# A pre-norm transformer block in fp32 on one core: the last 96 hidden features on four column tiles, and one batch's rows transposed through DRAM

## The chip, the core and the metric

The kernel runs on one core of a Trainium2 chip. Time is device microseconds (us) of one execution. The kernel before was run three times: 890.35, 890.20 and 889.15 us, median 890.2 us. One further execution was taken with the profiler; it lasted 889.38 us, of which 887.7 us lie between the first and the last instruction (the span).

## The reference, cut to what matters

```python
B, T, D = 4, 512, 512          # resid; 32 query heads and 8 key heads of 16; FF = 1376
x = resid
h = layernorm(x)
q, k, v = h @ Wq, h @ Wk, h @ Wv            # rotary embedding on q and k
probs = softmax(causal(q @ k.T / 4))        # four query heads share a key head
x = x + (probs @ v) @ Wo
h = layernorm(x)
x = x + (silu(h @ W_gate.T) * (h @ W_up.T)) @ W_down.T
```

All of it is fp32. The feed-forward layer has F = 1376 = 10 x 128 + 96 hidden features, so the last block of features is 96 wide.

## The kernel before, in words

**Layout.** A projection needs the normalised rows with features on the partitions (`xnT`, 128 x 4 x 512, one for a batch of 512 rows). There are two ways to turn rows round. `transposed` (L255) lets PE transpose four 128x128 blocks into a bank of PSUM, which ACT or DVE copies out. `flipped` (L265) lets DVE transpose 32x32 blocks of a 128x512 tile (`xt`, L268), then sends the tile to a DRAM buffer with four DMAs (L272) and brings finished columns back with one DMA for each 128 rows (L274); the call for the last row tile issues two such reads. All these DMAs are issued by SP, in program order, and so are the loads of input rows (L338, four of 256 KB for a batch), the writes and reads of row maxima (L640, L649, L651), and the feed-forward weights (L161).

**Attention.** Work goes in 32 groups, eight a batch: four heads that share the 32-row strips of PE. A group is computed twice: "plain" scores (queries on partitions, L553), of which DVE takes the greatest of each row (L599), and, two groups later, "less" scores (keys on partitions, L566) from which the maximum has been subtracted, for ACT's exponential (L654), POOL's causal mask (L659) and PE's weighted averages (`av`, L681). `slot(b, steps)` (L799) runs the eight groups of batch b. In one turn for group g it does five visits: visits n = 0 to 3 of the loop (L827) and `last_visit` (L848). Each visit issues plain scores of group g+2 and less scores of group g on PE, then the reduction of the plain scores on DVE; the next visit's plain scores use the same PSUM banks. Maxima are turned by DVE (L639) and go through DRAM.

**What fills the gaps.** `slot` also gets a list of steps (`steps`): PE work of the neighbouring batches, each with a planned cost, which `gap(n)` hands out after each visit by shares of the total. Small DVE, ACT and POOL steps wait in a queue `aside`; `odd_steps` (L225) hands them out after each visit's reductions, as many as fit a planned budget. For layernorm of batches 2 and 3 these are, for each of four row tiles: measure m (L200 to L203), normalise n (a small DVE step, L210, then ACT, L211) and flip f, in the order m0 m1 n0 m2 f0 n1 m3 f1 n2 n3 f2 f3 (L324). A step `tail(i)` (L414, the lists `turned`) makes sure that flip i has been handed out, by handing out from `aside` until it has. `begin` (L406) of a batch issues that batch's four input loads and appends its twelve steps to `aside`.

**Which batch turns how.** Batches 1 and 3 are flipped through DRAM buffer `flip[1]`; batches 0 and 2 are transposed by PE (the flag `b % 2`). Batch 2's layernorm is queued in the opening, before slot 0; in slot 0 the list is: rest of batch 1's projections with the four transposes of batch 2 woven into their last eight steps (`turns`, L880), then `begin3`, batch 2's projections, the waits for batch 3's flips, and most of batch 3's projections. `xt` tiles and the feed-forward's `g` tiles share two buffers (tag "g").

**Feed-forward.** `hidden(b, n)` (L483) computes, for each block f of features, two halves: gate (a = 0) and up (a = 1). A half is four products (contraction over 4 x 128 features) of `m` output features by 512 rows. In the slots `narrow` is set, and `product_of` (L248) splits a product into column tiles of 32 output features; after slot 3 (batch 3's feed-forward) a product is one 128-column matmul. For f = 10 the block is 96 wide, so three column tiles of 512 columns are used. An fp32 matmul appears in the trace as two passes. Gating is a tanh on ACT (L503) and two DVE operations (L504, L506) into `home`; `down` (L512) multiplies by W_down, block f = 10 last. `hidden` of batches 0, 1 and 2 runs in slots 1, 2 and 3 as filler.

Of the kernel before, what the change touches and what calls it, by code (L numbers as in the profile page):

```python
# [14 lines left out]
AF = mybir.ActivationFunctionType  # L15
ALU = mybir.AluOpType
# [5 lines left out]
P = 128  # L22
# [52 lines left out]
def preln_block_kernel(  # L75
# [172 lines left out]
    def product_of(out, lhsT, rhs, start, stop):  # L248
        if not narrow[0]:
            nc.tensor.matmul(out, lhsT=lhsT, rhs=rhs, start=start, stop=stop)  # L250
            return
        for c in range(0, out.shape[0], 32):
            nc.tensor.matmul(out[c : c + 32], lhsT=lhsT[:, c : c + 32], rhs=rhs, start=start, stop=stop)  # L253
# [11 lines left out]
    def flipped(xn, i, n, dst, last=NT - 1):  # L265

        t = work.tile([P, D], F32, tag="g", name="xt", bufs=2)
        nc.vector.transpose(t, xn)  # L268
        turned = flip[n].rearrange("(c d) (i r s) -> i r d c s", d=32, r=4, s=32)
        for r in range(4):  # L270
            rows = t[32 * r : 32 * r + 32, :]
            nc.sync.dma_start(out=turned[i, r], in_=rows.rearrange("d (c s) -> d c s", s=32))  # L272
        for a in [i - 1, i] if i == last else [i - 1] if i > 0 else []:
            nc.sync.dma_start(out=dst[:, :, ts(a, P)], in_=flip[n].rearrange("(k p) t -> p k t", p=P)[:, :, ts(a, P)])  # L274

    def portions(products, finish, n=2):

        made = {}

        def part(a):  # L280
            if a == 0:
                made["ps"] = bank()
            for step in products[len(products) * a // n : len(products) * (a + 1) // n]:
                step(made["ps"])
            if a == n - 1:
                full.append(deque(finish(made["ps"])))
                if not thin[0]:
                    emptied(len(full))

        return [lambda a=a: part(a) for a in range(n)]  # L290
# [22 lines left out]
    def both_steps(measure, norm, flip, tiles=range(NT), norm_us=0.6, flip_us=0.75):  # L313

        for i in tiles:
            yield 1.05, lambda i=i: measure(i)
            for a in [i - 1, i] if i == NT - 1 else [i - 1] if i > 0 else []:
                yield norm_us, lambda a=a: norm(a)
                yield flip_us, lambda a=a: flip(a)

    def both_steps_apart(measure, norm, flip, flip_us):

        steps = {"m": (1.05, measure), "n": (0.2, norm), "f": (flip_us, flip)}
        for kind, i in ("m0", "m1", "n0", "m2", "f0", "n1", "m3", "f1", "n2", "n3", "f2", "f3"):  # L324
            cost, step = steps[kind]
            yield cost, lambda step=step, i=int(i): step(i)

    def projections(b, n, early=False, then=None):

        home, xa, found, xn, ready = homes[n], {}, {}, {}, []  # L330
        xnT = xnT_of[b]

        def load(i):
            if early:
                xa[i] = xr[b, i]
            else:
                xa[i] = work.tile([P, D], F32, tag="xa", name="xa", bufs=4)
                nc.sync.dma_start(out=xa[i], in_=x[b, ts(i, P), :])  # L338

        def measure(i):  # L340
            found[i] = statistics(xa[i])

        def norm(i):
            xn[i] = work.tile([P, D], F32, tag="xa", name="xa", bufs=4) if early else xa[i]
            normalised(xn[i], found[i], by_act=b > 1)

        def flip(i):
            if b > 1:
                release()
            if b % 2:  # L350
                flipped(xn[i], i, 1, xnT)
            ready.append(i)
            if i == NT - 1 and then:
                then()

        def keys():
            def finish(ps):
                kr = work.tile([P, T], F32, tag="rot", name="kr", bufs=4)

                def spread():  # L360
                    release()
                    ks = work.tile([P, T], F32, tag="rot", name="ks", bufs=4)
                    nc.vector.stream_shuffle(ks, kr, SWAP)
                    for t, hf, src in ((0, 0, kr), (1, 1, kr), (0, 1, ks), (1, 0, ks)):
                        put(
                            lambda t=t, hf=hf, src=src: nc.gpsimd.tensor_scalar(
                                home[:, 4 + 2 * t + hf, :], src, halves[hf], (one16, one0)[hf], ALU.mult, ALU.add
                            )
                        )

                last = spread if early else lambda: soon.append((1, (0.75, spread)))
                return [*rotated(ps, kr, nc.vector if early else nc.gpsimd), (0.0, last)]

            return projected(wk_sb, 0, xnT, finish)

        def vals():
            def product(ps, i, k):
                for c in (0, 64) if i == NT - 1 else ():
                    token = P * i + 64 - c
                    product_of(  # L380
                        ps[c : c + 64, ts(i, P)], xnT[:, k, token : token + 64], wv_sb[:, k, :], k == 0, k == NK - 1
                    )
                if i < NT - 1:
                    product_of(ps[:, ts(i, P)], xnT[:, k, ts(i, P)], wv_sb[:, k, :], k == 0, k == NK - 1)

            def finish(ps):
                def copy():
                    nc.scalar.copy(
                        values(n)[:, :, :, DH : 2 * DH].rearrange("p i g d -> p (i g) d"),
                        ps.rearrange("p (a d) -> p a d", d=DH),  # L390
                    )

                return [(0.0, copy)]

            steps = [lambda ps, i=i, k=k: product(ps, i, k) for i in range(NT) for k in range(NK)]
            return [(0.45, step) for step in portions(steps, finish, 8)]

        def queries(m):
            engine = nc.vector if early and m == 0 else nc.gpsimd
            return projected(wq_sb, m, xnT, lambda ps: rotated(ps, home[:, m, :], engine))  # L400

        def load_all():
            for i in range(NT):
                load(i)

        def begin():  # L406
            if not xa:
                load_all()
            if b > 1:
                aside.extend(both_steps_apart(measure, norm, flip, 0.75 if b % 2 else 0.0))  # L410
            else:
                aside.extend(both_steps(measure, norm, flip, flip_us=0.75 if b % 2 else 0.0))

        def tail(i):  # L414
            while i not in ready:
                do(aside)
            if b % 2 == 0:
                transposed(xn[i], i, xnT)

        turned = [(0.0 if b % 2 else 0.45, lambda i=i: tail(i)) for i in range(NT)]  # L420
        rest = [*keys(), *queries(0), *vals()]
        for m in range(1, 4):
            rest += queries(m)
        return (0.0, begin), turned, rest, load_all
# [58 lines left out]
    def hidden(b, n):  # L483

        gs = {}

        def half(f, a):
            c = b * NF + f
            m = min(P, FF - f * P)

            def product(ps, k):
                if a == 0 and k == 0:
                    load_f(c + 2)
                product_of(ps[:m, :], wgu[c][:, a, k, :m], xnTs[0][:, k, :], k == 0, k == NK - 1)

            def finish(ps):
                return [(0.69, lambda: gated(ps))]

            def gated(ps):
                if a == 0:  # L500
                    gs[f] = work.tile([P, T], F32, tag="g", name="g", bufs=2)

                    nc.scalar.activation(gs[f][:m, :], ps[:m, :], AF.Tanh, scale=0.5)  # L503
                    nc.vector.scalar_tensor_tensor(gs[f][:m, :], gs[f][:m, :], 1.0, ps[:m, :], ALU.add, ALU.mult)  # L504
                else:
                    nc.vector.tensor_tensor(homes[n][:m, f, :], ps[:m, :], gs[f][:m, :], ALU.mult)  # L506

            return [(1.72, step) for step in portions([lambda ps, k=k: product(ps, k) for k in range(NK)], finish)]

        return [step for f in range(NF) for a in range(2) for step in half(f, a)]  # L510

# [365 lines left out]
    def restored():  # L877
        nc.scalar.dma_start(out=homes[1], in_=spill)

    turns = [step for pair in zip(turned2, *[iter(rest1[-8:])] * 2) for step in pair]  # L880
    slot(0, [*rest1[16:-8], *turns, begin3, *rest2, *turned3, *rest3[:-24]])

    before, behind = attended(0, by_pe=(2, 3))
    tiles = list(down(0, 0))
# [62 lines left out]
```

## Time and profile before

| what | value |
|---|---|
| median of three runs | 890.2 us (889.15 to 890.35) |
| the profiled execution | 889.38 us, span 887.7 us |
| PE, DVE, POOL, ACT busy | 865.9, 469.6, 233.7, 204.5 us |
| granted TensorE clock | 1.000 by the profile |
| chain of work that ended last | PE 81%, DVE 12%, POOL 3%, issue 2%, DMA 1%, ACT 1% |
| transposes by DVE for DRAM (L268) | 22, 0.71 us each |
| transposes by PE (L258) | 40, of these 16 for batch 2, at 79.1, 85.5, 88.2 and 90.8 us |
| first statistics of batch 3 (L200) | 95.69 us, right behind the DVE work before it |

How to read it: a line of the timeline gives start, duration, engine, line, operation, out<-in, shape and count, and in brackets how long the engine was idle and what ended that. "128*32 128x512" is a matmul with 128 rows of contraction, 32 output features and 512 columns. PE's ends are modelled, so starts are safer than ends. An SP line (SPq) is the time that SP took to issue DMAs, not the transfer.

First reductions of the groups in slot 0 (L599, 128x512) start at 51.58, 69.40, 85.65, 100.75, 116.17, 131.48, 147.65 and 162.75 us; slot 1 begins at 178.92 us. Slots 1 to 3 last until about 730 us, then follows batch 3's feed-forward.

### The profile page before, as it was taken

Reading aid. Unit: us, or ns where it says so; the run is one execution under the profiler, and the core shown is the slowest. Engines: PE = TensorE matmul, PEld = TensorE weight load, DVE = VectorE, ACT = ScalarE, POOL = GpSimd, SP = SyncE. Lnnn points to the kernel's source line nnn. Section 1 sums busy time; section 2 is a strip of 40 time slices with the busy share of each in tenths; the row PEclk is TensorE's granted clock in tenths of the full one; section 3 lists DMA queues with packets and bytes.
Section 4 is the critical chain, followed back from the end, with each engine's and each line's share of the span. In section 5 each row is a group of like instructions: output and inputs, shape, how many; then the busy total and the mean of one; then the engine's idle time right before and its main releaser. Section 6 shows DMA issues by size and latency. Waiting matters only on the chain.

```text
span 887.7 us, 23915 instructions
## 1 busy us (share of the span) xinstructions
PE 865.9 (98%) x10142; PEld 352.0 (40%) x10142; DVE 469.6 (53%) x1481; ACT 204.5 (23%) x256; POOL 233.7 (26%) x358
## 2 busy tenths in 40 slices
PE   6989999999999999999999999999999999999998
PEld 5654444544333333333333333333333334444443
DVE  7886788777555554485555544575555214121110
ACT  1024433322323222222222222122222220000100
POOL 5564475653212211132221122222211211000000
PEclk9999999999999999999999999999999999999999
DMA  8500114005515110524221110142111203523000
GB/s 247 133 5 4 52 16 87 4 4 121 180 50 178 44 50 14 192 51 110 55 57 50 31 40 25 52 98 73 51 50 50 68 13 84 130 71 83 18 13 35
DMA packets 122762, 59.68 MB, mean 67 GB/s; under 512 B 60480, under 2 KB 114752, under 8 KB 122400
## 3 DMA queue, kind: packets, MB, share of 16 engines
q1 hardware_dynamic: 122368, 52.39, 22.7%
q10 hardware_dynamic: 288, 5.77, 1.7%
q8 instruction: 80, 1.31, 0.6%
q14 instruction: 26, 0.21, 0.1%
HBM read 44.76 MB, written 13.37 MB: 65 GB/s over the span
## 4 chain that ended last, share of the span: by engine, by line
PE 81%; DVE 12%; POOL 3%; issue 2%; DMA 1%; ACT 1%; SPq 0%; POOLq 0%; DVEq 0%; ACTq 0%
PE mm L253 42%; PE mm L250 17%; PE sc L553 12%; DVE junk L599 6%; PE av L681 6%; PE sc L566 4%; POOL e L659 1%; DVE st L200 1%; DVE rot L304 1%; POOL qa L538 1%; ACT e L654 1%; DVE home L308 1%; DMA flip<-xt 0%; PE mm L258 0%; DVE xt L268 0%
## 5 line engine op out<-in xcount | busy, mean ns | idle before, releaser
L599 DVE CUSTOM_DVE_ANT_0 junk<-sc,mask 128x128 f32<-128x128 f32 (+3 forms) x512 | 251.1, 490 | 153.5 <-PE sc L566 94.6
L253 PE MATMUL mm<-xnT,shared 128*32 128x512 f32 (+1 forms) x2704 | 282.2, 545 | 1.0 <-DVE xnT L261 1.0
L654 ACT ACTIVATE e<-sc 128x1024 f32<-128x1024 f32 (+1 forms) x192 | 165.5, 882 | 411.7 <-PE sc L566 323.7
L659 POOL TENSOR_SCALAR_AFFINE_SELECT e<-e 128x512 f32<-128x512 f32 (+2 forms) x192 | 105.6, 560 | 365.5 <-ACT e L654 362.6
L553 PE MATMUL sc<-home,qa 32*64 32x512 f32 (+6 forms) x2048 | 158.7, 421 | 5.8 <-DVE low L599 3.0
L566 PE MATMUL sc<-qa,home 32*64 32x512 f32 (+6 forms) x2048 | 152.2, 427 | 2.7 <-DVE low L599 2.2
L253 PEld LDWEIGHTS mm<-xnT,shared 128*32 128x32 f32 x2704 | 88.0, 109 | 157.5 <-issue 142.1
L553 PEld LDWEIGHTS sc<-home,qa 32*64 32x64 f32 x2048 | 67.3, 131 | 109.0 <-issue 40.0
L250 PE MATMUL mm<-xnT,shared 128*128 128x512 f32 (+2 forms) x256 | 94.8, 529 | 0.0
L253 PE MATMUL mm<-wd_sb,home 128*32 128x512 f32 (+1 forms) x808 | 94.7, 594 | 0.0
L681 PE MATMUL av<-e,home 128*32 128x512 f32 (+3 forms) x1024 | 80.6, 437 | 1.4 <-POOL e L659 1.4
L504 DVE SCALAR_TENSOR_TENSOR g<-g,mm 128x512 f32<-128x512 f32 (+1 forms) x44 | 30.2, 687 | 96.6 <-ACT g L503 96.6
L566 PEld LDWEIGHTS sc<-qa,home 32*64 32x64 f32 x2048 | 58.7, 130 | 33.1 <-issue 13.4
L250 PEld LDWEIGHTS mm<-xnT,shared 128*128 128x128 f32 (+1 forms) x256 | 48.0, 190 | 46.6 <-issue 44.7
L503 ACT ACTIVATE g<-mm 128x512 f32<-128x512 f32 (+1 forms) x44 | 26.3, 597 | 168.8 <-PE mm L250 109.6
L250 PE MATMUL mm<-wd_sb,home 128*128 128x512 f32 (+1 forms) x150 | 65.0, 593 | 0.0
L506 DVE TENSOR_TENSOR home<-mm,g 128x512 f32<-128x512 f32 (+1 forms) x44 | 30.4, 690 | 57.3 <-PE mm L253 34.0
L522 DVE SCALAR_TENSOR_TENSOR xr<-mm,xr 128x512 f32<-128x512 f32 x16 | 11.0, 689 | 76.8 <-PE mm L250 56.2
L681 PEld LDWEIGHTS av<-e,home 128*32 128x32 f32 x1024 | 31.1, 109 | 44.8 <-issue 36.6
L253 PEld LDWEIGHTS mm<-wd_sb,home 128*32 128x32 f32 (+1 forms) x808 | 28.2, 110 | 50.6 <-issue 49.6
L253 PE MATMUL mm<-wo_sb,cx 128*32 128x512 f32 x384 | 45.0, 595 | 0.0
L250 PEld LDWEIGHTS mm<-wd_sb,home 128*128 128x128 f32 (+1 forms) x150 | 28.4, 190 | 36.3 <-issue 36.3
(73 smaller groups left out, 452.1 us busy)
## 6 DMA issues: line engine op xcount, KB each, us to landing
shared<-in_wg SPq DMA_DIRECT2D x40, 256.0 KB
shared<-in_wu SPq DMA_DIRECT2D x40, 256.0 KB
flip<-xt SPq DMA_DIRECT2D x88, 64.0 KB
xnT<-flip SPq DMA_DIRECT2D x18, 256.0 KB
xr<-in_x SPq DMA_DIRECT2D x16, 256.0 KB
out<-xr SPq DMA_DIRECT2D x16, 256.0 KB
xa<-in_x SPq DMA_DIRECT2D x12, 256.0 KB
spill<-wd_sb ACTq DMA_DIRECT2D x1, 2816.0 KB
```

The source lines that it names most:

```text
L250: nc.tensor.matmul(out, lhsT=lhsT, rhs=rhs, start=start, stop=stop)
L253: nc.tensor.matmul(out[c : c + 32], lhsT=lhsT[:, c : c + 32], rhs=rhs, start=start, stop=stop)
L503: nc.scalar.activation(gs[f][:m, :], ps[:m, :], AF.Tanh, scale=0.5)
L504: nc.vector.scalar_tensor_tensor(gs[f][:m, :], gs[f][:m, :], 1.0, ps[:m, :], ALU.add, ALU.mult)
L506: nc.vector.tensor_tensor(homes[n][:m, f, :], ps[:m, :], gs[f][:m, :], ALU.mult)
L522: nc.vector.scalar_tensor_tensor(xr[b, i], py[i], 0.5, xr[b, i], ALU.mult, ALU.add)
L553: nc.tensor.matmul(dst[at : at + 64, :n], lhsT=qa[g][rows_of(r), q : q + 64], rhs=keys_of(g)[rows_of(r), :n], start=True, stop=True,)
L566: nc.tensor.matmul(dst[at : at + 64, first_q:], lhsT=keys_of(g)[rows_of(r), k : k + 64], rhs=qa[g][rows_of(r), P * j + first_q :], start=True,
L599: nc.vector.tensor_tensor_reduce(out=junk[:, :n], in0=src, in1=mask[:, T - n : T] if i else mask[:, T:], scale=-1.0, scalar=BIG, op0=ALU.a ...
L654: nc.scalar.activation(dst, src, AF.Exp, scale=1.0 / math.sqrt(DH))
L659: nc.gpsimd.affine_select(out=e[rows, heads, c : c + P], in_=e[rows, heads, c : c + P], compare_op=ALU.is_ge, fill=0.0, base=base, pattern ...
L681: nc.tensor.matmul(av[32 * r : 32 * r + 32, P * j :], lhsT=v[:, j, 4 * (m // 2) + r, DH * (1 - hf) : DH * (3 - hf)], rhs=e[:, r, c : c + n ...
```

## The change

Two edits.

1. Block f = 10 of `hidden`: column tiles 0 to 2 compute the 96 features for the first 384 rows only; column tile 3 (partitions 96 to 127 of the bank) computes the last 128 rows, for one 32-feature strip after the other, in three stretches of 128 columns. So each product issues three matmuls of 384 columns and three of 128, in place of three of 512 (or of one of 96 features by 512 columns in batch 3). Gating then works on 128 partitions by 384 columns, and three DMAs of 32x128, issued by SP behind the last DVE operation, move the results of tile 3 to their partitions in `home`. The step's planned cost goes from 1.72 to 1.29.

2. Batch 2 is flipped through DRAM (`flip[0]`) like batches 1 and 3, instead of transposed by PE. Its four flips are planned at 0.75 each; the `turned2` steps cost 0. In slot 0 they come four steps earlier and in one piece, directly followed by `begin3`; the last twelve steps of batch 1's projections now come behind `begin3`.

```diff
--- before.py
+++ after.py
@@ -347,8 +347,8 @@
         def flip(i):
             if b > 1:
                 release()
-            if b % 2:
-                flipped(xn[i], i, 1, xnT)
+            if b > 0:
+                flipped(xn[i], i, b % 2, xnT)
             ready.append(i)
             if i == NT - 1 and then:
                 then()
@@ -407,17 +407,17 @@
             if not xa:
                 load_all()
             if b > 1:
-                aside.extend(both_steps_apart(measure, norm, flip, 0.75 if b % 2 else 0.0))
+                aside.extend(both_steps_apart(measure, norm, flip, 0.75))
             else:
-                aside.extend(both_steps(measure, norm, flip, flip_us=0.75 if b % 2 else 0.0))
+                aside.extend(both_steps(measure, norm, flip, flip_us=0.75 if b else 0.0))
 
         def tail(i):
             while i not in ready:
                 do(aside)
-            if b % 2 == 0:
+            if b == 0:
                 transposed(xn[i], i, xnT)
 
-        turned = [(0.0 if b % 2 else 0.45, lambda i=i: tail(i)) for i in range(NT)]
+        turned = [(0.0 if b else 0.45, lambda i=i: tail(i)) for i in range(NT)]
         rest = [*keys(), *queries(0), *vals()]
         for m in range(1, 4):
             rest += queries(m)
@@ -487,11 +487,34 @@
         def half(f, a):
             c = b * NF + f
             m = min(P, FF - f * P)
+            most = T - P
+            cols = slice(0, T if m == P else most)
 
             def product(ps, k):
                 if a == 0 and k == 0:
                     load_f(c + 2)
-                product_of(ps[:m, :], wgu[c][:, a, k, :m], xnTs[0][:, k, :], k == 0, k == NK - 1)
+                if m == P:
+                    product_of(ps, wgu[c][:, a, k, :], xnTs[0][:, k, :], k == 0, k == NK - 1)
+                    return
+
+
+                for q in range(3):
+                    at = slice(32 * q, 32 * q + 32)
+                    nc.tensor.matmul(
+                        ps[at, :most],
+                        lhsT=wgu[c][:, a, k, at],
+                        rhs=xnTs[0][:, k, :most],
+                        start=k == 0,
+                        stop=k == NK - 1,
+                    )
+                for q, kq in (divmod(n, NK) for n in range(3 * k, 3 * k + 3)):
+                    nc.tensor.matmul(
+                        ps[96:P, ts(q, P)],
+                        lhsT=wgu[c][:, a, kq, 32 * q : 32 * q + 32],
+                        rhs=xnTs[0][:, kq, most:],
+                        start=kq == 0,
+                        stop=kq == NK - 1,
+                    )
 
             def finish(ps):
                 return [(0.69, lambda: gated(ps))]
@@ -500,12 +523,17 @@
                 if a == 0:
                     gs[f] = work.tile([P, T], F32, tag="g", name="g", bufs=2)
 
-                    nc.scalar.activation(gs[f][:m, :], ps[:m, :], AF.Tanh, scale=0.5)
-                    nc.vector.scalar_tensor_tensor(gs[f][:m, :], gs[f][:m, :], 1.0, ps[:m, :], ALU.add, ALU.mult)
+                    g = gs[f][:, cols]
+                    nc.scalar.activation(g, ps[:, cols], AF.Tanh, scale=0.5)
+                    nc.vector.scalar_tensor_tensor(g, g, 1.0, ps[:, cols], ALU.add, ALU.mult)
                 else:
-                    nc.vector.tensor_tensor(homes[n][:m, f, :], ps[:m, :], gs[f][:m, :], ALU.mult)
-
-            return [(1.72, step) for step in portions([lambda ps, k=k: product(ps, k) for k in range(NK)], finish)]
+                    nc.vector.tensor_tensor(homes[n][:, f, cols], ps[:, cols], gs[f][:, cols], ALU.mult)
+                    for q in range(3) if m < P else ():
+                        nc.sync.dma_start(
+                            out=homes[n][32 * q : 32 * q + 32, f, most:], in_=homes[n][96:P, f, ts(q, P)]
+                        )
+
+            return [(1.72 if m == P else 1.29, step) for step in portions([lambda ps, k=k: product(ps, k) for k in range(NK)], finish)]
 
         return [step for f in range(NF) for a in range(2) for step in half(f, a)]
 
@@ -877,8 +905,7 @@
     def restored():
         nc.scalar.dma_start(out=homes[1], in_=spill)
 
-    turns = [step for pair in zip(turned2, *[iter(rest1[-8:])] * 2) for step in pair]
-    slot(0, [*rest1[16:-8], *turns, begin3, *rest2, *turned3, *rest3[:-24]])
+    slot(0, [*rest1[16:-12], *turned2, begin3, *rest1[-12:], *rest2, *turned3, *rest3[:-24]])
 
     before, behind = attended(0, by_pe=(2, 3))
     tiles = list(down(0, 0))
```

Built, the order of instructions changes as follows around the second edit (read from the built program, group 1 of slot 0 being the one that begins at 69.40 us in the trace of before). On DVE, f0 stands in the last but one visit of group 0, f1 behind the reductions of visit 1 of group 1, and n3, f2 and f3 behind those of visit 2; behind those of visit 3 stand m0 of batch 3 and the two DVE operations of a rotation (L304, L308), then `last_visit`. f3 waits for the DMAs of f1, whose `xt` buffer it takes. On SP the order is: four DMAs of f1, read 0, four of f2, read 1, four of f3, reads 2 and 3, and then the four loads of batch 3's rows. Before, these loads stood behind the reads of maxima of the next group (issued at 89.11 us), and m0 of batch 3 in visit 3 of group 2.

## The prediction

> **What bounds the kernel now.** I read the page first, then the chain in order of time, stage by stage.
>
> ```profile
> PE 865.9 (98%) x10142; PEld 352.0 (40%) x10142; DVE 469.6 (53%) x1481; ACT 204.5 (23%) x256; POOL 233.7 (26%) x358
> ```
>
> PE looks like the bound everywhere, but its ends are modelled, so the chain decides. In slot 0 and in slot 2 it reads:
>
> ```profile
> 152.93 0.56 DVE junk L599
> 153.53 0.56 DVE junk L599
> 154.13 0.29 DVE junk L599
> 154.46 0.29 DVE junk L599
> 154.81 0.52 PE sc L553 x2
> 155.34 0.26 PE sc L553 x2
> 155.93 0.56 DVE junk L599
> ...
> 428.61 2.38 PE av L681 x32
> 430.99 3.43 PE mm L253 x32
> 435.47 3.57 PE mm L253 x32
> ...
> 729.94 153.88 PE mm L250 x358
> ```
>
> In slot 0 (51.6 to 178.9 us) reductions on DVE and scores on PE take turns: neither can run ahead, because both use the same banks. From slot 1 on everything listed is PE. So PE time taken out of slots 1 to 3 or of the end is gained in full; in slot 0 PE filler is nearly free, and DVE work or a DVE wait beyond a small slack is paid.
>
> **Edit 1, the column tiles.** From the timeline of PE:
>
> ```profile
> 325.40 3.63 PE L253 MATMUL mm<-xnT,shared 128*32 128x512 f32 x24
> 339.55 3.64 PE L253 MATMUL mm<-wd_sb,home 128*32 128x512 f32 x32
> 167.86 1.96 PE L253 MATMUL mm<-shared,xnT 128*32 128x128 f32 x64
> ```
>
> The first is block 10 on three tiles (24 passes, 8 rounds), the second 8 rounds on four tiles: same time, so column tiles run beside each other and the fourth was idle. A round of 512 columns is 3.43 / 8 = 0.43 us; a product is two, 0.86, a half of four products 3.43. The third line is 16 rounds of 128 columns, one behind the other on each tile: (1.96 - 0.27 for the last one's duration) / 15 = 0.11 each. After the change tiles 0 to 2 need 2 x 0.43 x 384/512 = 0.64 a product and tile 3 six passes of 0.11 = 0.66. A half: 4 x 0.66 = 2.64, a gain of 0.79. Six halves in slots 1 to 3: 4.7. In the last stage 16 passes of L250 at 153.88 / 358 = 0.43 (6.9 us) become 2 x 2.64, less two changes of shape at 0.14 each (3.57 from start to start above, against 3.43): 1.3. Together **-6.0 us**. Bounds: 0 if the unequal pieces do not overlap; -6.9 if a pass takes its columns' share alone (8 x 0.86).
>
> The other parts of edit 1 are hidden. Tanh and gating get shorter off the chain. The three copies for each batch cost SP's issue time and a transfer like the maxima's, but `down` reads them only in block 10 of its fourth row tile, over 25 us of PE work (three tiles of 11 x 0.86) later; what stands behind them on SP, weights and maxima, waits no longer than for a DVE operation that those maxima follow on DVE anyway. Without that cover it would be one landing, some 2 us, a batch.
>
> One rule speaks against edit 1. In the score timeline second passes of 320 columns start at 324.81, before the second passes of 384 columns at 324.84 that belong to matmuls issued earlier, so tiles seem to run independently. The Trainium skill ("TensorE: Matmul & The Clock Gate", Part 3, The mechanism) says that matmuls start and end strictly in program order; then each stretch on tile 3 would hold up the next product, and by that rule the gain would be nil and the sum 9 us over before.
>
> **Edit 2, what goes.** PE's 16 transposes of batch 2 (four at 0.66, with the change of shape) and four ACT copies (0.58). Group 2, which holds three of the four, took 85.65 to 100.75 = 15.1 us, as long as group 6, which has none (147.65 to 162.75). So they cost nothing now, and their going gains nothing.
>
> **Edit 2, what it adds.** Four DVE transposes, sixteen flip DMAs, four reads, and earlier loads of batch 3's rows behind them on SP. The rows:
>
> ```profile
> 142.23 0.70 DVE L268 STREAM_TRANSPOSE xt<-xa 128x512 f32<-128x512 f32 x1
> ```
> ```profile
> 89.11 2.70 SPq L338 DMA_DIRECT2D xa<-in_x  x4
> ...
> 142.97 1.99 SPq L272 DMA_DIRECT2D flip<-xt  x4
> 145.07 3.11 SPq L274 DMA_DIRECT2D xnT<-flip  x2
> 148.23 0.50 SPq L640 DMA_DIRECT2D lowest<-turned  x1
> ```
> ```profile
> DVE xr L449 <- DMA xr<-in_x: 4.3, 1, 4.3
> ```
>
> SP needs about half a microsecond to issue one DMA, and the second of the last two reads waits for the last flip to land: it went out at 147.80, that is 4.9 us after its transpose ended. The waits' line shows that DVE does stand still when a load it needs is late. A load of rows took 2.2 us from issue at 89.11 to the end of its packets (91.3 in the trace), and 3.0 in another place (37.85 to 40.85).
>
> Now group 1 after the change, on the times of before. Visit 1's reductions end at 74.6; f1 is done at 75.3, its DMAs are issued until 77.4 and land at about 78.9. Visit 2's reductions end at 77.6; f2 runs to 78.4; f3 needs f1's buffer, starts at 78.95 and ends at 79.65. SP issues f2's DMAs from 78.4 to 80.4, read 1 to 80.9, f3's DMAs to 83.0, read 2 to 83.5, and read 3 when f3 has landed, between 85.0 and 85.8. Then the first load: issue from 85.4 to 86.2, data at 87.6 to 89.2. I take 88.2.
>
> DVE reaches m0 of batch 3 much earlier: visit 3's reductions start at 79.65 instead of 78.74 and end at 81.5. It then **waits 6.7 us** (5.6 at least: 4.9 + 0.4 issue + 2.2 landing behind f3, less 1.83 of reductions; 8.6 if the two reads still hold the DMA engines). Queued behind m0 are its own 1.03, a rotation of 1.23, and last_visit's reductions, for which the next group's scores on PE wait. Those reductions start at 88.2 + 1.03 + 1.23 = 90.45; to the next group's first reduction it is 3.15 as before (82.50 to 85.65): 93.6 instead of 85.65, **+7.95**.
>
> The remaining visits: a visit hides about 1.2 us of extra DVE work (0.02 idle at 1.23 extra, at 150.32). After the change two visits of group 3 exceed it (0.96 + 1.23 in the first, 2.1 in the fourth, where the exponential hides more: 0.95 + 0.3), while the surplus of group 5 (147.65 - 131.48 = 16.17, against 15.1) and of group 3 (0.3) goes, and group 0 loses a statistics step's POOL work on its chain (0.4). Sum about -0.5 (+1 to -1.5).
>
> The clock: PE has its averages done about 85 and waits for DVE until about 92. The only comparable idle time in the trace is the beginning:
>
> ```profile
> 6.23 1.11 PE L258 MATMUL mm<-ident,xa 128*128 128x128 f32 x4 [6.23 <-DVE xa L213]
> ...
> 79.14 0.66 PE L258 MATMUL mm<-ident,xa 128*128 128x128 f32 x4
> ```
>
> After 6.2 us of nothing the same four transposes take 1.11 in place of 0.66, and passes become fast at about 11.7. If the same happens here, a visit's scores (0.8 to 0.9) take about twice as long in the first two or three visits of group 2, part of it behind DVE: +1.5 us (0 if PE stays fast, 3 if nothing hides it). I take 1.5, since the idle time is as long as the one at the beginning. The Trainium skill ("TensorE: Matmul & The Clock Gate", Part 1, What's actually happening) has PE fall to half clock after an idle window of 3.4 us, which agrees; the profile's clock column reads 1.00 throughout and shows neither.
>
> **Sum.** Slot 0: 7.95 - 0.5 + 1.5 = +8.95. Column tiles: -6.0. Net +2.95 us on the profiled execution's 889.38, 892.3; that execution lies 0.8 below the median of the runs, so against 890.2 it is **893.1 us**.
>
> **Rivals.** (a) *PE keeps its clock.* For it: no row shows a drop in mid-kernel. Against: the beginning. 893.1 - 1.5 = 891.6, no measurable difference. (b) *Unequal column tiles do not overlap.* For it: before has no three stretches on one tile beside one long one on others. Against: the scores' passes above. Then 890.2 + 8.95 = 899.1. (c) *The wait is covered, and the kernel gets faster.* The place is m0 of batch 3 behind visit 3 of group 1: if its rows are there when DVE asks, slot 0 costs 7.95 - 6.7 - 0.5 = +0.75 and PE never idles long: 890.2 + 0.75 - 6.0 = 885.0. Faster by 0.2% (1.8 us, about what a measurement of this kernel can tell from no change) needs a wait under 3.5 us at full clock. For it: only the built order, no row, speaks for the wait, and group 1's own times may shift. Against: 4.9 + 0.4 + 2.2 alone leave 5.6.
>
> **Chances.** Forecast 0.54 (0.50 slower, 0.04 same); (a) 0.20 (0.16 same, 0.04 slower); (b) 0.15, slower; (c) 0.11 (0.09 faster, 0.02 same). So faster 0.09, same 0.22, slower 0.69. The range goes from 888.8 (a with the shortest wait, 1.1 less, the visits' best and some of the tiles' bound: 891.6 - 1.1 - 1.0 - 0.7) to 899.5 (b); it leaves out (c) and the dearest ends.
>
> **What would show it.** Right: in block 10 24 passes of 384 and 24 of 128 columns within 2.7 us a half; on DVE an idle time of 5.6 to 8.6 before a statistics step at about 82 to 88, ended by the DMA of input rows; PE idle as long, and then scores at half rate; slot 1 beginning 7 to 10 us later than 178.9 and the last matmul 1 to 4 later. Wrong: no such idle time (then c), or block 10 as long as before (then b).

## The result and the profile after

The changed kernel takes 892.85 us (median of seven runs, 890.51 to 893.60); the kernel before took 889.43 us beside it (seven runs, 889.06 to 890.35). The ratio is 1.0029, with a 95% interval from 1.0017 to 1.0042, so the change is slower: by 3.4 us between the medians, by 2.6 us if one takes the ratio. The profiled execution of the changed kernel lasted 890.95 us, its span is 889.2 us. (In the new file the lines after the edit are shifted by 28: reductions are L627, scores L581 and L594, averages L709, masks L687. The two new matmuls are L503 and L511.)

The page's busy times, and the shares of the chain that ended last:

```profile
PE 857.5 (96%) x10350; PEld 363.5 (41%) x10350; DVE 470.5 (53%) x1485; ACT 202.2 (23%) x252; POOL 233.1 (26%) x358
...
PE 80%; DVE 11%; DMA 3%; POOL 2%; issue 2%; SPq 1%; ACT 0%; POOLq 0%; DVEq 0%; ACTq 0%
```

PE has 8.4 us less to do than before, and yet the span is longer; DMA (3% in place of 1%) and SP's queue now stand in the chain. More of these parts lies between 73 and 91 us than anywhere else, and this is the place to look at.

**Where time came in.** The waits' view of DVE (us in total, times, longest) now has this line:

```profile
DVE st L200 <- DMA xa<-in_x: 8.2, 1, 8.2
```

The timeline of DVE shows where it is. Each line is start, duration, engine, line, operation, and in brackets the idle time before it and what ended that:

```profile
76.11 0.70 DVE L268 STREAM_TRANSPOSE xt<-xa 128x512 f32<-128x512 f32 x1
77.86 0.71 DVE L268 STREAM_TRANSPOSE xt<-xa 128x512 f32<-128x512 f32 x1 [1.05 <-DMA flip<-xt]
...
80.22 0.08 DVE L627 DVE_READ_ACCUMULATOR2_ANT low<- 128x1 f32 x1
88.45 0.69 DVE L200 BATCH_NORM_STATS2 st<-xa 128x6 f32<-128x512 f32 x1 [8.16 <-DMA xa<-in_x]
...
90.68 0.42 DVE L627 CUSTOM_DVE_ANT_0 junk<-sc,mask 128x256 f32<-128x256 f32 x1
...
94.62 0.69 DVE L627 CUSTOM_DVE_ANT_0 junk<-sc,mask 128x512 f32<-128x512 f32 x1 [0.87 <-PE sc L594]
```

DVE ends visit 3 of group 1 at 80.3 and then stands for 8.16 us, because the next operation in its queue is the first statistics step of batch 3, and its rows are not there. Behind it stand the reductions of `last_visit` (90.68), and the next group's first reduction comes at 94.62 instead of 85.65. The timeline of SP says why the rows are late:

```profile
73.71 2.54 SPq L272 DMA_DIRECT2D flip<-xt  x4
76.35 0.45 SPq L274 DMA_DIRECT2D xnT<-flip  x1
76.90 2.10 SPq L272 DMA_DIRECT2D flip<-xt  x4
79.11 0.43 SPq L274 DMA_DIRECT2D xnT<-flip  x1
79.59 2.25 SPq L272 DMA_DIRECT2D flip<-xt  x4
82.00 3.26 SPq L274 DMA_DIRECT2D xnT<-flip  x2
85.30 1.93 SPq L338 DMA_DIRECT2D xa<-in_x  x4
```

SP issues almost without a pause from 73.7 on; its pair of reads at 82.00 holds it for 3.26 us, since the second of them waits for the last flip to land. The loads of rows come only then.

Compare this with before. There the loads went out at 89.11, and their reader came at 95.69. The change issues the loads 3.8 us earlier, but DVE comes to their reader 15 us earlier (at 80.3). So the loads are late for a reader that has moved forward, and the flips ahead of them on SP keep them from moving as far.

PE stands as well, and its clock falls. First its timeline, then the windows view (stretch, length, then busy time and count for PE, PEld, DVE, ACT and POOL, the granted clock, the DMA share and GB/s):

```profile
81.30 1.93 PE L709 MATMUL av<-e,home 128*32 128x512 f32 x24
90.68 1.42 PE L709 MATMUL av<-e,home 128*32 128x256 f32 x8 [7.45 <-POOL e L687]
92.03 1.12 PE L581 MATMUL sc<-home,qa 32*64 32x512 f32 x2
...
96.11 0.65 PE L581 MATMUL sc<-home,qa 32*64 32x512 f32 x2
```
```profile
82.00:86.00 4.00, 1.23 (x20) 0.39 (x12) 0.00 (x0) 0.58 (x2) 0.00 (x0) 1.00 0.53 109
86.00:90.00 4.00, 0.00 (x0) 0.00 (x0) 1.48 (x5) 0.00 (x0) 0.30 (x1) 0.68 0.95 313
90.00:94.00 4.00, 3.32 (x24) 0.99 (x24) 3.47 (x13) 0.00 (x0) 3.92 (x6) 0.50 0.06 18
94.00:98.00 4.00, 3.88 (x63) 1.33 (x56) 3.32 (x9) 1.61 (x2) 2.02 (x3) 0.96 0.01 2
```

The same pass of 512 columns takes 1.12 us at 92.03 and 0.65 at 96.11. The windows give the clock that goes with it: 1.00, then 0.68 as a mean (that is 0.5 for the last 2.6 us of the stretch, so from 87.4 on), 0.50, and back at about 94.3.

**Where time went out.** Block 10 in the timeline of PE:

```profile
336.86 0.52 PE L503 MATMUL mm<-xnT,shared 128*32 128x384 f32 x3
336.88 0.52 PE L511 MATMUL mm<-xnT,shared 128*32 128x128 f32 x3
337.20 0.50 PE L503 MATMUL mm<-xnT,shared 128*32 128x384 f32 x3
337.23 0.49 PE L511 MATMUL mm<-xnT,shared 128*32 128x128 f32 x3
```

Three passes of 384 columns and three of 128 start together every 0.32 to 0.34 us. Eight such rounds are a half: 2.60 us where it was 3.43.

To sum up by stages I take the first averages (`av`) of the first group that a slot works on as its beginning; "the last averages" are the first ones of the last group:

| stage | before | after | first edit alone (e1) |
|---|---|---|---|
| slot 0 | 130.40 us | 139.14 | 130.45 |
| slot 1 | 186.81 | 182.89 | 182.72 |
| slot 2 | 188.98 | 188.10 | 188.12 |
| slot 3, to the last averages | 155.83 | 154.12 | 154.15 |
| from there to the last matmul | 158.00 | 156.71 | 156.70 |

Slot 0 gives 8.7 us away, the rest gains 7.8. That is 0.9 us on balance; the profiled executions differ by 1.57 (890.95 - 889.38), and the medians by 3.4. These views don't show where the rest of the medians' difference lies; the clocks of the single runs (last section) bear on it.

### The profile page after: what moved, and what is told of

It is laid out like the page before. It is cut to its first block, busy times and chain, and to the rows that moved or that the text cites. A ratio compares the mean times of both kernels' runs of the same rounds, so it can differ in the third digit from the quotient of the medians.

```text
span 889.2 us, 24381 instructions
## 1 busy us (share of the span) xinstructions
PE 857.5 (96%) x10350; PEld 363.5 (41%) x10350; DVE 470.5 (53%) x1485; ACT 202.2 (23%) x252; POOL 233.1 (26%) x358
## 4 chain that ended last, share of the span: by engine, by line
PE 80%; DVE 11%; DMA 3%; POOL 2%; issue 2%; SPq 1%; ACT 0%; POOLq 0%; DVEq 0%; ACTq 0%
PE mm L253 39%; PE mm L250 17%; PE sc L581 12%; DVE junk L627 6%; PE av L709 6%; PE sc L594 4%; PE mm L511 2%; DMA flip<-xt 1%; SPq L272 1%; PE mm L503 1%; POOL e L687 1%; DVE st L200 1%; POOL qa L566 1%; DMA shared<-in_wg 1%; DVE home L308 0%
## 5 line engine op out<-in xcount | busy, mean ns | idle before, releaser
L627 DVE CUSTOM_DVE_ANT_0 junk<-sc,mask 128x128 f32<-128x128 f32 (+3 forms) x512 | 251.1, 491 | 156.5 <-PE sc L594 93.2
L253 PE MATMUL mm<-xnT,shared 128*32 128x512 f32 (+1 forms) x2560 | 260.5, 542 | 1.2 <-DMA shared<-in_wg 1.2
L687 POOL TENSOR_SCALAR_AFFINE_SELECT e<-e 128x512 f32<-128x512 f32 (+2 forms) x192 | 105.2, 557 | 364.3 <-ACT e L682 361.3
L581 PE MATMUL sc<-home,qa 32*64 32x512 f32 (+6 forms) x2048 | 158.8, 423 | 8.2 <-DVE low L627 5.7
L594 PE MATMUL sc<-qa,home 32*64 32x512 f32 (+6 forms) x2048 | 153.0, 428 | 2.8 <-DVE low L627 2.1
L253 PEld LDWEIGHTS mm<-xnT,shared 128*32 128x32 f32 x2560 | 82.5, 109 | 144.3 <-issue 130.8
L581 PEld LDWEIGHTS sc<-home,qa 32*64 32x64 f32 x2048 | 67.3, 131 | 110.3 <-issue 37.2
L250 PE MATMUL mm<-xnT,shared 128*128 128x512 f32 (+1 forms) x240 | 88.2, 526 | 0.0
L709 PE MATMUL av<-e,home 128*32 128x512 f32 (+3 forms) x1024 | 80.3, 439 | 8.1 <-POOL e L687 8.1
L594 PEld LDWEIGHTS sc<-qa,home 32*64 32x64 f32 x2048 | 58.8, 130 | 31.4 <-issue 12.1
L250 PEld LDWEIGHTS mm<-xnT,shared 128*128 128x128 f32 x240 | 45.7, 192 | 42.5 <-issue 40.4
L709 PEld LDWEIGHTS av<-e,home 128*32 128x32 f32 x1024 | 31.0, 109 | 50.9 <-issue 37.4
```

What stands on the lines that cost most here:

```text
L581: nc.tensor.matmul(dst[at : at + 64, :n], lhsT=qa[g][rows_of(r), q : q + 64], rhs=keys_of(g)[rows_of(r), :n], start=True, stop=True,)
L594: nc.tensor.matmul(dst[at : at + 64, first_q:], lhsT=keys_of(g)[rows_of(r), k : k + 64], rhs=qa[g][rows_of(r), P * j + first_q :], start=True,
L627: nc.vector.tensor_tensor_reduce(out=junk[:, :n], in0=src, in1=mask[:, T - n : T] if i else mask[:, T:], scale=-1.0, scalar=BIG, op0=ALU.a ...
L687: nc.gpsimd.affine_select(out=e[rows, heads, c : c + P], in_=e[rows, heads, c : c + P], compare_op=ALU.is_ge, fill=0.0, base=base, pattern ...
L709: nc.tensor.matmul(av[32 * r : 32 * r + 32, P * j :], lhsT=v[:, j, 4 * (m // 2) + r, DH * (1 - hf) : DH * (3 - hf)], rhs=e[:, r, c : c + n ...
```

## The experiments

My theory: the column tiles gain what PE's time says; the flips of batch 2 cost nothing themselves, but they delay the loads of batch 3's rows on SP, and DVE's wait for these and the clock that falls meanwhile are the whole loss. Times are medians; the kernel before ran beside each: 889.79 us beside e1 to e4, 889.73 beside the others.

**e1, the first edit alone** (the second undone):

```diff
-    slot(0, [*rest1[16:-12], *turned2, begin3, *rest1[-12:], *rest2, *turned3, *rest3[:-24]])
+    turns = [step for pair in zip(turned2, *[iter(rest1[-8:])] * 2) for step in pair]
+    slot(0, [*rest1[16:-8], *turns, begin3, *rest2, *turned3, *rest3[:-24]])
```
with the five conditions on `b` in `flip`, `begin`, `tail` and `turned` as before.

> Edit 1 alone (batch 2 is transposed by PE as before). My theory: the column tiles give 0.83 us in each of six halves in the slots and 1.5 us in the last stage, about 6.5 to 7.8 us in all: 882.4 us (881.4 to 883.2), slot 0 as long as before (slot 1 begins at 178.9). Rival: part of the 7.8 us that the changed kernel wins back behind slot 0 is only its delay being caught up, and the tiles alone are worth 5 or less: 884.4 or more.

Measured: 881.88 us (881.32 to 882.49), ratio 0.9912 [0.9899, 0.9926]. So the first edit alone, tiles and planned cost together, is worth 7.9 us, and this version beats both kernels.

**e2, the second edit alone** (the mirror of e1: block 10 as before).

> Edit 2 alone (block 10 on three column tiles as before). My theory: the wait for batch 3's first rows, about 8 us, and a slow PE behind it push slot 1 from 178.9 to 187 or 190 and all of it reaches the end: 899 us (897 to 901.5). Rival (delay caught up in slot 1): 895 or less, with slot 1 shorter than before.

Measured: 899.11 us (897.22 to 899.72), ratio 1.0102 [1.0088, 1.0116]; the second edit alone costs 9.3 us. The wait is there without any column tiles:

```profile
DVE st L200 <- DMA xa<-in_x: 8.6, 1, 8.6
```

**e3, the first rows early.** Everything as in the changed kernel, but tile 0 of batch 3's rows takes a buffer from another set (tag "xr") and is loaded at the beginning of slot 0; the other three tiles are loaded where they were. The cut shows the two main places.

```diff
-                xa[i] = work.tile([P, D], F32, tag="xa", name="xa", bufs=4)
+                own = b == 3 and i == 0
+                xa[i] = work.tile([P, D], F32, tag="xr" if own else "xa", name="xa", bufs=6 if own else 4)
...
+    slot(0, [after(load3), *rest1[16:-12], *turned2, begin3, ...
```

> The changed kernel, with batch 3's first row tile in a buffer of its own and loaded at the beginning of slot 0, so that its load is not behind the flips on SP; the order of everything on DVE and PE stays. My theory: the 8 us wait and the half clock go, the DVE transposes stay and cost 1 us or less: 883.2 us (882 to 884.5), slot 1 beginning at 179 to 180.5. Rival (it is the added DVE work, the flips' DMAs and SP's queue themselves that cost): 888 or more, slot 1 still beginning after 185.

Measured: 883.13 us (882.64 to 883.71), ratio 0.9926 [0.9914, 0.9938]. In the timeline of DVE the statistics follow at once, though the twelve flip DMAs from 74.0 on are all still there, and the next group begins at 86.53:

```profile
81.14 0.08 DVE L629 DVE_READ_ACCUMULATOR2_ANT low<- 128x1 f32 x1
81.14 0.69 DVE L200 BATCH_NORM_STATS2 st<-xa 128x6 f32<-128x512 f32 x1
```

Slot 0 lasts 130.36 us, as before the change. One load in time takes the whole loss of slot 0 away.

**e4, the wait without the half clock.** 60 extra matmuls of 32 features by 256 columns in group 1 keep PE busy; they write into the averages' bank, which is overwritten afterwards.

```diff
+        for q in range(60 if g == 1 else 0):
+            nc.tensor.matmul(av[32 * (q % 4) : 32 * (q % 4) + 32, : 2 * P], lhsT=wo_sb[:, 0, ts(q % 4, 32)],
+                             rhs=wo_sb[:, 1, : 2 * P], start=True, stop=True)
```

> The changed kernel with 60 extra matmuls of 32x256 on PE (6.5 us at full clock, their result is overwritten) ahead of group 1's averages, inside the time in which PE idles. The wait on DVE stays. My theory: PE keeps its full clock, so group 2 starts at full rate; the time falls by 1 to 3 us to about 890.7 (889.7 to 891.7), the runs lie within 1 us of each other, and the mean granted clock is 1.000. Rival (the half clock is hidden behind DVE, or the spread of the runs has another cause): no change from 892.9, the same spread of some 3 us.

Measured: 890.74 us (890.37 to 894.30, 11 runs), ratio 1.0020 [1.0011, 1.0029]. DVE waits as long, but the clock stays at 1.00 and the scores are fast:

```profile
DVE st L200 <- DMA xa<-in_x: 8.1, 1, 8.1
```
```profile
81.97 6.68 PE L707 MATMUL av<-wo_sb 128*32 128x256 f32 x120
...
93.30 0.65 PE L594 MATMUL sc<-qa,home 32*64 32x512 f32 x2
```

So in the profiled execution a busy PE keeps its clock, while the wait stays. What the half clock costs is less certain: the medians lie 892.85 - 890.74 = 2.1 us apart, the two profiled executions 0.5 (890.95 and 890.42), and the ratios to the kernel before, 1.0029 and 1.0020, 0.8, with intervals that overlap. One expectation failed: the runs were to lie within 1 us at a mean clock of 1.000. They spread over 3.9 us, as much as those of the changed kernel, with clocks of 0.997 to 1.000 (890.37 to 892.17 in the nine at 0.999 or more). At least a part of the spread has another cause, which stays open.

After these four, 1.5 us of the gain of e1 had no explanation (six halves at 0.83 and 1.3 to 1.5 at the end are 6.3 to 6.5, not 7.9). Two kernels take the planned cost apart from the passes.

**e5, the first edit with the old planned cost**

```diff
-            return [(1.72 if m == P else 1.29, step) for step in portions(...
+            return [(1.72, step) for step in portions(...
```

> The first edit alone, but with the planned cost of block 10's steps left at 1.72 instead of 1.29. The first edit alone gave 881.9 us, 7.9 less than before, of which the passes explain 6.3 to 6.5 (six halves at 0.83, the last stage 1.3 to 1.5). Theory P, the planner: the remaining 1.5 us comes from where the cheaper steps let the gaps hand out the other steps (before, PE stands 0.67 us at 212.4 and 0.22 at 398.7 ahead of scores, which the first edit alone doesn't show). With the old cost it is gone again: 883.4 us (883.0 to 883.9). Rival Q, the passes: the matmuls themselves gain more than their timeline shows; the cost doesn't matter: 881.9 us (881.6 to 882.3).

Measured: 882.96 us (882.65 to 883.47), ratio 0.9923 [0.9909, 0.9936]. That is just under the planner's range and well over the rival's; all runs of e5 are longer than all of e1.

**e6, the kernel before with the new planned cost and nothing else** (the same line the other way round, at L508).

> The kernel before with the planned cost of block 10's steps at 1.29 and nothing else. Theory P, the planner: the idle times of PE at 212.4 and 398.7 go, with up to 1.5 us: 888.3 us (888.0 to 888.9) beside 889.8 for before. Rival Q, the passes: 889.8 us, the same as before.

Measured: 888.11 us (887.68 to 889.27, 11 runs), ratio 0.9982 [0.9973, 0.9991]. Between the profiled executions, from slot 1 to the last matmul, e5 is 6.4 us shorter than before, e6 1.5, and e1, with both, 7.9: they add up. The planner's part is real. How it comes about is seen in the timeline of DVE, first before (with the scores that follow on PE), then e6:

```profile
210.59 0.67 DVE L308 TENSOR_TENSOR wd_sb<-mm,rope_sb 128x512 f32<-128x512 f32 x1
211.18 0.54 DVE L599 CUSTOM_DVE_ANT_0 junk<-sc,mask 128x384 f32<-128x384 f32 x1
...
213.06 0.54 PE L553 MATMUL sc<-home,qa 32*64 32x384 f32 x2 [0.67 <-DVE low L599]
```
```profile
210.18 0.55 DVE L599 CUSTOM_DVE_ANT_0 junk<-sc,mask 128x384 f32<-128x384 f32 x1
...
211.93 0.73 DVE L304 STREAM_SHUFFLE rot<-mm 128x512 f32<-128x512 f32 x1
```

Before, a rotation stands ahead of the visit's reductions, and PE's next scores wait 0.67 us for these (at 213.06; 0.22 at 398.94 in slot 2). Since the gaps share out the planned total, a smaller total makes them hand out a little less each; the rotation falls behind the reductions, where it holds up nothing, and both waits are gone; in e5 both are back. These account for 0.9 of the 1.5 us; I have not located the rest.

**e7, begin3 behind the last projections of batch 1** (in the changed kernel):

```diff
-    slot(0, [*rest1[16:-12], *turned2, begin3, *rest1[-12:], *rest2, ...
+    slot(0, [*rest1[16:-12], *turned2, *rest1[-12:], begin3, *rest2, ...
```

> The changed kernel with begin3 behind the last twelve steps of batch 1's projections instead of ahead of them: the loads of batch 3's rows are issued later, but its first statistics step is handed out about a group of slot 0 later still. Theory, the wait of DVE for late rows is the cost of the second edit, and only its place in the order makes it: no idle time of DVE before L200, no half clock, 882.7 us (882.0 to 884.0), that is the first edit alone plus at most the 1.2 us that DVE's extra work cost when the first rows were loaded early. Rival, the traffic of the flips delays whatever load comes behind it, and the wait moves to group 2 with the statistics step: 887 to 891 us.

Measured: 882.77 us (882.20 to 883.42), ratio 0.9920 [0.9906, 0.9934]. From SP's and DVE's timelines:

```profile
92.60 3.02 SPq L338 DMA_DIRECT2D xa<-in_x  x4
```
```profile
96.76 0.69 DVE L200 BATCH_NORM_STATS2 st<-xa 128x6 f32<-128x512 f32 x1
```

The loads go out 7.3 us later than in the changed kernel, and nothing waits, because their reader has moved further: DVE comes to it at 96.76, and not at 80.3. So the second edit without the early `begin3` costs at most 0.9 us (against e1); the loss needs `begin3` ahead as well as the flips on SP.

**e8, the rows loaded by ACT.** The built order is the same on every engine; only the four loads change from SP to ACT.

```diff
-                nc.sync.dma_start(out=xa[i], in_=x[b, ts(i, P), :])
+                (nc.scalar if b == 3 else nc.sync).dma_start(out=xa[i], in_=x[b, ts(i, P), :])
```

> The changed kernel with the four loads of batch 3's rows issued by ACT instead of SP; every other instruction stands where it stood on its engine. On ACT the loads follow the normalisation of batch 2's last row tile, at about 78, where SP issues them from 85.3. Theory S, the rows are late because SP issues them behind four flips' DMAs and a read that waits for the last flip: the first rows are there by about 82 and DVE waits 1 to 2 us in place of 8.2, PE doesn't fall to half clock; 883 to 885 us. Rival D, the transfers: the flips take the DMA engines themselves (the busy share of the 16 engines is 1.0 from 78 to 82 us and 0.6 to 84 in the changed kernel), so loads issued earlier move beside them and are done at 84 to 87; DVE waits 4 to 6 us: 887 to 890 us.

Measured: 881.61 us (880.49 to 883.33), ratio 0.9909 [0.9896, 0.9923]. ACT's timeline, then DVE's:

```profile
76.50 4.49 ACTq L338 DMA_DIRECT2D xa<-in_x  x4
81.04 1.02 ACT L682 ACTIVATE e<-sc 128x1024 f32<-128x1024 f32 x1 [3.73 <-DVE xt L268]
```
```profile
79.92 0.71 DVE L268 STREAM_TRANSPOSE xt<-xa 128x512 f32<-128x512 f32 x1 [2.83 <-DMA flip<-xt]
...
82.27 0.69 DVE L200 BATCH_NORM_STATS2 st<-xa 128x6 f32<-128x512 f32 x1
```

DVE's wait for rows is gone altogether; the theory had left 1 to 2 us of it, and a time of 883 to 885. What made the rows late was their place behind the flips on SP, not the traffic. The rival may have a small share: f3's wait for f1's buffer grows from 1.05 to 2.83 us beside the loads; in e3, without loads beside it, it was 1.66. ACT pays too: the loads wait there for batch 2's buffers, and an exponential stands behind them for 3.73 us. The time lies with e1, e3 and e7, from 881.6 to 883.1. The Trainium skill ("Perfetto Trace Analysis", DMA Optimizations) says that balancing DMAs over the engines that can issue them may help where generating their descriptors, and not moving the data, is the bottleneck. e8 agrees in part: 11.2 us lie between the medians of the changed kernel and of e8, but SP's queue was held not by issuing alone, but also by a read that waited for a landing (the 3.26 us at 82.00).

## Why the prediction was right, and where its sizes were off

The direction, the place and the mechanism held, and the predicted 893.1 us is 0.25 over the median. But that closeness is partly luck: three sizes were off, and they cancel, and the kernel before, taken at 890.2, measured 889.43 beside the changed one.

| term | predicted | measured |
|---|---|---|
| slot 0 without the half clock | 7.95 - 0.5 = +7.45 us | +8.9 (e4 - e1) |
| half clock | +1.5 | +2.1 by medians, +0.5 by profiled executions (changed kernel - e4) |
| column tiles | -6.0 | -7.9 (e1) |
| sum | +2.95 | +3.1 by medians (beside 889.79 for before; +3.4 beside 889.43) |

The measured column adds up because its terms are differences of the same four medians; the sum is no check of them. Two others are. By the stages of e4's profiled execution slot 0 is 8.6 us longer than before (139.02 against 130.40), which bears the first row out. And e2, the second edit with its half clock, costs 9.3 us, where the first two rows add up to 11.0 by the medians and to 9.4 with the profiled half clock.

- **DVE's wait** was put at 6.7 us and took 8.16. Its end was nearly right (rows at 88.2; they came at 88.45), its beginning was not: I had visit 3's reductions end at 81.5, and they ended at 80.3. The step took group 1's times from before. There, visit 1's reductions stood 2.30 us for scores and began at 73.13; in the changed order PE has 16 filler passes ahead of those scores (at 68.85) instead of 24 (at 69.29), and they begin at 71.63. A DVE that comes earlier to a fixed arrival waits longer. (`last_visit` was predicted at 90.45 and came at 90.68.)
- **From the rows to the next group's reduction** I took 5.4 us; e4 shows 5.37 (89.08 to 94.45), the changed kernel 6.17 (88.45 to 94.62); the 0.8 more goes with scores at half rate.
- **What idled PE.** The prediction had PE finish its averages at about 85. They did not finish: the last eight passes came at 90.68, released by POOL's mask (L687). That mask stands on POOL behind the last part of the statistics step (L203), which waited for the same rows. A wait on DVE had held a second queue, which I had not followed. In POOL's timeline:

```profile
89.70 0.55 POOL L203 TENSOR_TENSOR rstd<-rstd,neghalf 128x1 f32<-128x1 f32 x1 [9.34 <-DVE rstd L202]
90.22 0.76 POOL L687 TENSOR_SCALAR_AFFINE_SELECT e<-e 128x256 f32<-128x256 f32 x2
```

- **The half clock** came, as forecast, and rival (a) fell. Its length is not fixed: in the profiled execution it lasted 6.9 us (87.4 to 94.3), and its cost there is small (890.95 against 890.42 for e4's profiled execution); by the medians it is 2.1. The 1.5 lies between, and the runs don't settle it.
- **The other visits** (-0.5): e3 has all of the second edit's DVE work without the wait. It is 1.25 us over e1 by the medians, but by the stages of the profiled executions only 0.2 (812.4 us against 812.1 from the first averages to the last matmul). The prediction's figure for this case, +0.75, lies between; more can't be told.
- **Column tiles.** The passes give 6.4 by e5's profiled execution (6.8 by its median), close to the 6.0, with 2.60 us a half for 2.64. The other 1.5 (1.1 to 1.6 by the medians) is the planned cost (e6), to which the prediction gave no price at all: it listed the cost of 1.29 as a part of the change and left it there. So the sum of 7.9 lies outside its bounds of 0 to 6.9.
- **Rival (b)**, no overlap of unequal tiles, is refuted by block 10's timeline and by e1. In it the second passes of 384 columns (337.20) start after passes of 128 columns (336.88) that belong to matmuls issued later. The Trainium skill ("TensorE: Matmul & The Clock Gate", Part 3, The mechanism) states a strict order of matmuls; for these, of two passes each, it does not hold as the prediction read it, and the measurement decides.
- **Rival (c)**, the covered wait, was the right description of e3, e7 and e8: 885.0 was its price, with the tiles too low by 1.9; they measured 883.1, 882.8 and 881.6.

## What to carry to other kernels

When transfers are added to a queue, list what is behind them in that queue, and for each the moment at which somebody needs it: here a step moved ahead brought the reader of a load forward by 15 us, while the load, behind the added flips in its queue, came forward by only 4, and DVE, POOL and PE stood for it in turn. The remedy is in the order, not in the amount: an earlier load, a later reader or another issuing engine each took the loss away. And a planned cost is part of a change: price what it moves, even where it only says truly what a step now takes.

## What the runs showed of the hardware beyond the expectation

- The length of the clock's fall differs from run to run: 6.9 us in the profiled execution of the changed kernel, 10.2 in that of e2 (86.9 to 97.1, by the windows of its clock), and, as an estimate from the mean clocks of the changed kernel's runs (0.996 to 0.992), 7 to 14 us. In that kernel it goes with the time: runs with a mean clock of 0.996 took 890.51 to 891.64 us, those with 0.994 and 0.993 892.85 to 893.17, the one with 0.992 893.60. That it alone makes the time is not shown: a longer wait could lengthen both; of e2's runs two with 0.996 took 897.22 and 899.08; and e4's runs spread as far at 0.997 to 1.000. The Trainium skill ("TensorE: Matmul & The Clock Gate", Part 1, What's actually happening) says that the gate watches a free-running window, so that the same kernel meets it at different phases; lengths that differ between runs of one kernel agree with this.
- PE stood 7.45 us in the changed kernel, and the clock fell 4.2 us after its last matmul (83.2 to 87.4); in e2 it stood 7.88 us, and the clock fell after 3.3 (83.6 to 86.9). In e8 it stood 3.1 us (79.3 to 82.4), and the clock stayed at 1.00.
- Three stretches of 128 columns on one column tile run wholly beside 384 columns on the three others: a round of 0.32 us is 0.75 of the 0.43 for 512 columns, so the shorter stretches cost nothing.
